# Two layers with adaptive norms on one core: layer 0's units ordered by batch row instead of by group

## The chip, the cores and the metric

One NeuronCore of a Trainium2 chip runs the whole computation in one program. The metric is the device time of one execution in microseconds, the median of several runs; one more execution was profiled. Everything is float32; where a matmul has to be exact, both operands are split into a rounded high part and a low remainder, and three fast matmuls (high-high, high-low, low-high) stand for one.

## The reference

Two layers are applied to x, two batch rows of 512 tokens with 512 channels. Each layer has an attention part and a feed-forward part, each behind a layer norm whose scale, shift and output gate come from a conditioning vector:

```python
mod = (silu(c) @ wmod).reshape(2, 6, 1, 512)          # sa, ca, ga, sb, cb, gb
h = layernorm(x) * (1 + ca) + sa;  x = x + ga * attn(h)
h = layernorm(x) * (1 + cb) + sb;  x = x + gb * ffn(h)
```

Layer 0's attention is a gated linear attention: 32 heads of 128 channels in 8 groups that share keys and values. A decay per token and head is worked out from h (`softplus(h @ Win.T + dt_bias)` times `-exp(A_log)`, summed up within chunks of 128 tokens). In each chunk the scores are weighted with the decays; a state of 128 x 128 per head is carried from chunk to chunk; the output is normalised, gated with `silu(h @ Wg.T)` and projected with `Wo`. Its feed-forward is one matmul with signs of a weight, times a scale, plus a bias.

Layer 1's attention is softmax attention with 32 heads of 16 channels over 512 tokens. Its feed-forward mixes four streams of 128 channels with a 4 x 4 matrix per token that 50 rounds of Sinkhorn normalisation make. The batch rows never meet.

## The kernel before

**Units.** Layer 0's attention is cut into 64 units; a unit is a group g of four heads, a batch row b and a chunk c of 128 tokens. Four units with the same g and b are a step. A list written out by hand gives the order of the steps: groups 0 to 3 alternate between the rows (group 0 row 0, group 0 row 1, group 1 row 0, ...), then come groups 4 to 7 of row 0, then groups 4 to 7 of row 1 (`AHEAD = 4`). So row 0 is finished at unit 47.

A pass of the loop over units issues: the scores of the next unit (`scores`, which fetches the summed decays `gb` from DRAM, spread over all partitions), the mix of this one (`mix`: `yps`, normalisation, gate `sg`), keys, queries and values of the next step (`project`, matmuls `pps`, rotation in `apply_rope`), the output projection of the unit before (`project_out`, 12 matmuls `ops`, added to the residual `xres`), the next unit's gate (`gps`), its state (`cps`), and the turned output (`ztp`, `zh`, `zl`).

**Weights.** A group needs 14 tiles of 128 x 512: `wk`, `wv`, four each of `wq`, `wg`, `wo`. Each is fetched by a DMA on SyncE's queue into a tile of the pool `raw` (four buffers), copied and rounded by ScalarE to the high part, and subtracted by GpSimd to the low part (lines 210 and 211), which frees the raw tile. With `raw_tile` other loads use the same pool: pieces of the modulation matrices (`mod_piece`: fetch two or four tiles, and at the next piece multiply those of the last one, `mps`), the feed-forward weight, the residual input. While rows alternate, a set of weights serves two steps, 8 units; in groups 4 to 7 one step.

**Decays.** `decays(b)` normalises the four tiles of a row, turns them (`ps_tr`), makes `hh` and `hl`, multiplies with `Win` (`zps`) and then works along rows of 32 partitions (lines 381 to 420): softplus, a running sum in 15 + 7 small adds, exponentials, three sets of transposes (`gtp`). It is called for row 0 ahead of the first keys and for row 1 after the first queries.

**Beside the units.** `tail(n)` is called in each pass. It issues modulation pieces at n % 8 in 3 to 6, and, once a row's units have all been projected, the feed-forward of that row in eight or nine passes: layer norm and modulation of tile c, sums, feed-forward of tile c - 2 (`fps`), layer 1's norm of tile c - 3, and at the end the key, value and query projections of layer 1. For row 0 these are passes 45 to 53, its weights coming from pass 42. The tail of row 1 goes on behind the last unit, in `virtual` passes.

**Layer 1.** 128 pieces (16 steps of 8). A piece issues two score matmuls with their row maxima (`maxima`, `s`, `m`), and ten pieces later the weights and exponentials for the same keys (`weigh`, `pt`); every four pieces make a quad, whose outputs (`op`) and division (`rc`) follow. From `FIRST = 53` on each unit's pass issues three pieces, up to `HOLD = 33`; the rest follow the last unit. Behind every eighth quad starts a Sinkhorn job (`streams`) for two tiles, which runs beside the further pieces; the last one ends the kernel.

**Order.** The instructions of every engine are put in order before the run by a list scheduler; priorities follow the order in the program, and `anchor`/`behind` tie work beside the units to its phase. On the chip every engine, SyncE with its DMA issues included, works its list strictly in order.

Of the kernel before, what the change touches and what calls it, by code (L numbers as in the profile page):

```python
# [12 lines left out]
PT, OUT = 16, 1  # L13
S1, S2, MT, OT, OP = 3, 3, 2, 2, 2
QS = 6
HOLD = 33
VECTOR = False, False, True, True
UPS = 400, 400, 400, 400
RATES = None, None, None, None
# [5 lines left out]
HL, RA, ZL, XC, XP = 0, 0, 100, 100, 1  # L25
UPO = 600
SPLIT0, SPLIT1 = 16, 16
AHEAD = 4
FIRST = 53
PER = 3  # L30
LATE, LATE1 = 2, 12
LAG = 10
# [5 lines left out]
P = 128  # L38
# [15 lines left out]
def tile_adaln(ctx: ExitStack, tc: tile.TileContext, a: dict, out: bass.AP):  # L54
# [5 lines left out]
    wk = ctx.enter_context(tc.tile_pool(name="wk", bufs=2))  # L60
    dram = ctx.enter_context(tc.tile_pool(name="dram", bufs=1, space=bass.MemoryType.DRAM))
    psp = ctx.enter_context(tc.tile_pool(name="ps", bufs=2, space=PSUM))


    table = nc.scalar.preload_act_table_set("natural_log_exp_and_others")
# [105 lines left out]
    def norm(src):  # L171
        xn = temp([P, HID], FP, "xn")
        normalised(xn, src)
        return xn
# [190 lines left out]
    cdb = keep([P, B * H0, NC])  # L365
    g_dram = [dram.tile([H0, L], FP, name=f"g_dram{b}") for b in range(B)]
    cd_dram = [dram.tile([H0, NC], FP, name=f"cd_dram{b}") for b in range(B)]
    def decays(b):

        zps = psp.tile([H0, L], FP, name="zps")  # L370

        def also(cs, ht):
            for kc in range(KC):
                nc.tensor.matmul(zps[:, cs], lhsT=win[:, kc, :], rhs=ht[:, kc, :], start=kc == 0, stop=kc == KC - 1)

        for c in range(NC):
            modulated(b, c, norm(xin[b * NC + c]), modT[0], 0, also=also)

        row = lambda n: temp([H0, L], FP, n)
        z, e, u, rest, dt = row("z"), row("e"), row("u"), row("rest"), row("dt")  # L380
        nc.vector.tensor_scalar(z, zps, dtb, None, ALU.add)
        nc.vector.scalar_tensor_tensor(e, z, -1.0, z, ALU.mult, ALU.min)
        act(e, e, AF.Exp)

        nc.vector.tensor_scalar(u, e, 1.0, None, ALU.add)
        nc.vector.scalar_tensor_tensor(rest, u, -1.0, e, ALU.add, ALU.subtract)
        act(dt, u, AF.Ln)
        act(u, dt, AF.Exp, scale=-1.0)
        nc.vector.tensor_tensor(rest, rest, u, ALU.mult)
        nc.vector.tensor_tensor(dt, dt, rest, ALU.subtract)  # L390
        nc.vector.scalar_tensor_tensor(dt, z, 0.0, dt, ALU.max, ALU.add)

        G = row("G")
        nc.vector.tensor_scalar(G, dt, alog, -1.0, ALU.mult, ALU.mult)
        Gb = G.rearrange("r (n i) -> r n i", i=16)
        for i in range(1, 16):
            nc.vector.tensor_tensor(Gb[:, :, i], Gb[:, :, i], Gb[:, :, i - 1], ALU.add)
        off = small.tile([H0, NC, 8], FP, name="off")
        G4 = G.rearrange("r (c n i) -> r c n i", n=8, i=16)
        nc.vector.memset(off[:, :, 0], 0.0)  # L400
        for n in range(1, 8):
            nc.vector.tensor_tensor(off[:, :, n], off[:, :, n - 1], G4[:, :, n - 1, 15], ALU.add)
        nc.vector.tensor_tensor(
            Gb, Gb, off.rearrange("r c n -> r (c n)").unsqueeze(2).to_broadcast([H0, NC * 8, 16]), ALU.add
        )
        nc.sync.dma_start(out=g_dram[b], in_=G)
        Gc = G.rearrange("r (c i) -> r c i", c=NC)
        glast = small.tile([H0, NC], FP, name="glast")
        nc.vector.tensor_copy(glast, Gc[:, :, P - 1])
        cd = small.tile([H0, NC], FP, name="cd")  # L410
        act(cd, glast, AF.Exp)
        nc.sync.dma_start(out=cd_dram[b], in_=cd)
        nc.sync.dma_start(out=cdb[:, b * H0:(b + 1) * H0, :], in_=cd_dram[b].partition_broadcast(P))

        nc.vector.tensor_tensor(
            e.rearrange("r (c i) -> r c i", c=NC), Gc, glast.unsqueeze(2).to_broadcast([H0, NC, P]), ALU.subtract
        )
        act(e, e, AF.Exp, scale=-1.0)
        nc.vector.tensor_tensor(e, e, dt, ALU.mult)
        nc.vector.tensor_scalar(G, G, -1.0, None, ALU.mult)  # L420
        for k, src in enumerate((G, dt, e)):
            tp = psp.tile([P, NC, H0], FP, name="gtp")
            for c in range(NC):
                nc.tensor.transpose(tp[:, c, :], src[:, c * P:(c + 1) * P], ident[0:H0, 0:H0])
            nc.scalar.copy(gcol[:, k, :, b * H0:(b + 1) * H0], tp)
# [261 lines left out]
    def project_q(b, t):  # L687
        rope_halves("wq1", t, t, b, q_dram[b][8 * t:8 * t + 8], (0, 16), (32,))

    ends = [(KV0 - AHEAD) * B * NC + AHEAD * NC - NC + 1, KV0 * B * NC - NC + 1]  # L690

    def tail(n):

        if n % 8 in (3, 4, 5, 6) and n < 40:
            mod_piece(load=n % 8 < 6)

        for b in range(B):
            c = n - ends[b]
            with behind():
                if -3 <= c < 1:  # L700
                    load_ffn(c + 3)
# [44 lines left out]
                ksd[j, s] = temp([P, L], FR, f"ks{j}{s}")  # L746
                nc.sync.dma_start(out=ksd[j, s].bitcast(FP), in_=empty.bitcast(FP))

    steps = [(g, b) for g in range(KV0 - AHEAD) for b in range(B)]
    steps += [(g, b) for b in range(B) for g in range(KV0 - AHEAD, KV0)]  # L750
    units = [{"at": (g, b, c)} for g, b in steps for c in range(NC)]

    def keys_of(s):
# [510 lines left out]
    for hh in range(REP0):  # L1264
        load_stationary("wq0", 0, hh)
    nc.sync.dma_start(out=rope, in_=a["c_rope0"].rearrange("p (k l) -> p k l", k=2))
    load_x(1)
    load_stationary("wv0", 0, 0)
    load_gate(0)
    load_out(0)  # L1270
    decays(0)
    keys_of(0)
    for hh in range(REP0):
        query_of(0, hh)
    vT = values_of(0)
    decays(1)
    scores(units[0])
    values_turned(0, vT)
    units[1]["st"] = state(units[0], None)
# [151 lines left out]
```

## Time and profile before

| | us |
|---|---|
| median of 3 runs | 1403.43 (1400.64 to 1406.42) |
| profiled execution, its own time | 1409.56 |
| span in the profile | 1407.8 |
| TensorE busy / VectorE busy | 1247.3 / 1164.4 |
| ScalarE busy / GpSimd busy | 825.1 / 787.2 |
| first output projection of layer 0 (unit 0, unit 32, unit 44) | at 109.8, 539.1, 691.7 |
| first score matmul of layer 1 | at 898.4 |
| end of layer 0's units | at about 1046 |
| sixteenth quad of layer 1 done (all of row 0) | at 1157 |
| last quad done | at 1279 |

PE is TensorE, PEld its weight loads, DVE VectorE, ACT ScalarE, POOL GpSimd, SP SyncE. The page has 40 slices of 35.2 us; a digit is the busy share in tenths. In lines of the stretches every engine's busy microseconds are followed by the number of its instructions. In lines of waits the total of the waits is followed by their number and the longest.

### The profile page before, as it was taken

What the parts mean: (1) busy time and instruction counts of PE and PEld (TensorE: products, weight loads), DVE (VectorE), ACT (ScalarE), POOL (GpSimd) and SP (SyncE); (2) the same over time, 40 slices, a digit from 0 to 9 for tenths busy, and PEclk for the clock granted to TensorE, in tenths of its full rate; (3) what the DMA queues carried; (4) which work ended last, traced back from release to release, by engine and by line L of the source; (5) the groups of instructions that cost most, each with busy time, mean ns of one, the idle gap of its engine ahead of it and who ended that gap; (6) DMA issues with size and microseconds to landing.
All of it is one profiled execution on the core that took longest, in us unless ns stands there. A gap on an engine that the chain in (4) does not pass through costs nothing. (4 is left out here: it accounts for less than half of the span.)

```text
span 1407.8 us, 23038 instructions
## 1 busy us (share of the span) xinstructions
PE 1247.3 (89%) x7128; PEld 990.5 (70%) x7128; DVE 1164.4 (83%) x3171; ACT 825.1 (59%) x2333; POOL 787.2 (56%) x1180
## 2 busy tenths in 40 slices
PE   6979999999999999999988998899998899994117
PEld 3767888788788778888876777677776667762116
DVE  7998668687677687787999977788699879888998
ACT  5456576476476466666665655567567467653226
POOL 4363274365264367577777757644243644657854
PEclk9999999999999999999999999999999899986568
DMA  7121241231131233224333327623212331100001
GB/s 241 36 70 43 87 124 39 68 106 53 53 118 56 94 117 111 81 79 128 120 106 90 98 70 233 179 66 97 65 42 94 101 92 48 59 2 1 1 15 46
DMA packets 95378, 117.14 MB, mean 83 GB/s; under 512 B 10828, under 2 KB 50508, under 8 KB 95256
## 3 DMA queue, kind: packets, MB, share of 16 engines
q1 hardware_dynamic: 95256, 115.67, 27.6%
q8 instruction: 57, 0.93, 0.3%
q14 instruction: 65, 0.53, 0.1%
HBM read 102.11 MB, written 10.64 MB: 80 GB/s over the span
## 5 line engine op out<-in xcount | busy, mean ns | idle before, releaser
L847 DVE TENSOR_REDUCE m<-s 128x1 f32<-128x512 f32 x256 | 166.6, 673 | 21.8 <-PE s L843 21.5
L68 ACT ACTIVATE pt<-s 128x512 f32<-128x512 f32 x256 | 137.4, 601 | 33.1 <-PE s L877 31.5
L448 POOL TENSOR_TENSOR q<-xcos,rot 128x512 f32<-128x512 f32 x64 | 92.8, 1450 | 56.5 <-DVE xcos L446 52.5
L68 ACT ACTIVATE sg<-sg 128x512 f32<-128x512 f32 x128 | 80.7, 632 | 64.5 <-DVE sg L479 62.5
L496 POOL TENSOR_SCALAR_AFFINE_SELECT dec<-gb 128x512 f32<-128x512 f32 x64 | 48.3, 755 | 121.2 <-DMA gb<-g_dram 65.4
L843 PE MATMUL s<-ks,qs 96*128 96x512 f32 x256 | 104.9, 442 | 11.5 <-DVE m L847 7.6
L877 PE MATMUL s<-qs,ks 100*128 100x256 f32 x512 | 104.4, 309 | 10.2 <-DMA qs<-mm 6.8
L233 PE MATMUL pps<-hh,wq_h 128*128 128x512 f32 x256 | 103.3, 403 | 7.1 <-ACT vT L767 3.4
L877 PEld LDWEIGHTS s<-qs,ks 100*128 100x128 f32 x512 | 82.7, 199 | 32.8 <-issue 7.9
L68 ACT ACTIVATE dec<-dec,room 128x128 f32<-128x128 f32 x256 | 83.0, 398 | 34.8 <-POOL dec L496 34.6
L233 PE MATMUL ops<-wo_h,zh 128*128 128x512 f32 x256 | 102.2, 399 | 1.2 <-ACT zh L571 1.0
L233 PE MATMUL gps<-wg_h,hh 128*128 128x512 f32 x256 | 101.3, 398 | 1.5 <-ACT wg_h L210 1.2
L233 PE MATMUL ops<-wo_h,zl 128*128 128x512 f32 x256 | 101.5, 396 | 0.7 <-DVE zl L572 0.7
L233 PE MATMUL pps<-hl,wq_h 128*128 128x512 f32 x256 | 101.8, 398 | 0.0
L233 PE MATMUL pps<-hh,wq_l 128*128 128x512 f32 x256 | 101.5, 397 | 0.0
L233 PE MATMUL gps<-wg_l,hh 128*128 128x512 f32 x256 | 101.1, 395 | 0.0
L233 PE MATMUL ops<-wo_l,zh 128*128 128x512 f32 x256 | 100.6, 393 | 0.0
L233 PE MATMUL gps<-wg_h,hl 128*128 128x512 f32 x256 | 100.6, 393 | 0.0
L516 POOL TENSOR_TENSOR gb<-gb,q 128x512 f32<-128x512 f32 x48 | 62.3, 1299 | 60.3 <-ACT gb L68 46.7
L549 PE MATMUL yps<-v,dec 128*128 128x128 f32 x512 | 93.4, 278 | 2.7 <-DVE xcos L446 1.4
L555 ACT ACTIVATE z<-yps 128x128 f32<-128x128 f32 x256 | 67.5, 278 | 41.1 <-PE yps L551 30.5
L559 DVE SCALAR_TENSOR_TENSOR z<-yps,ss,sg 128x128 f32<-128x128 f32 x256 | 72.0, 340 | 22.5 <-ACT ss L68 22.3
(321 smaller groups left out, 3984.4 us busy)
## 6 DMA issues: line engine op xcount, KB each, us to landing
gb<-g_dram SPq DMA_DIRECT2D x64, 256.0 KB
raw<-in_wq SPq DMA_DIRECT2D x56, 256.0 KB
raw<-in_wg SPq DMA_DIRECT2D x48, 256.0 KB
raw<-in_wo SPq DMA_DIRECT2D x48, 256.0 KB
raw<-in_wmod SPq DMA_DIRECT2D x40, 256.0 KB
qs<-q_dram SPq DMA_DIRECT2D x64, 96.0 KB
q_dram<-hi SPq DMA_DIRECT2D x16, 256.0 KB
raw<-in_wk SPq DMA_DIRECT2D x14, 256.0 KB
```

The lines of the kernel that those rows point to most:

```text
L68: ins = nc.scalar.activation(o, i, func, **kw)
L233: nc.tensor.matmul(ps, lhsT=l, rhs=r, start=i == 0, stop=i == n - 1)
L448: nc.gpsimd.tensor_tensor(dst, sp(xc_), sp(rot), ALU.add)
L496: anchor["pool"] = nc.gpsimd.affine_select(out=dec, in_=gb, pattern=[[0, REP0], [1, P]], compare_op=ALU.is_ge, fill=-1e30, base=0, channel ...
L516: nc.gpsimd.tensor_tensor(gb, gb, q[:, c], ALU.mult)
L549: nc.tensor.matmul(yps[:, h, :], lhsT=u["pr"][:, h, :], rhs=u["v"][:, c, :], start=True, stop=not c)
L555: nc.scalar.activation(z[:, h, :], yps[:, h, :], AF.Square, accum_out=ss[:, h:h + 1])
L559: nc.vector.scalar_tensor_tensor(z[:, h, :], yps[:, h, :], ss[:, h:h + 1], sg[:, h * P:(h + 1) * P], ALU.mult, ALU.mult)
L843: anchor["pe"] = nc.tensor.matmul(ps, lhsT=st["qs"][rp][0:KS, i, qt * P:(qt + 1) * P], rhs=st["ks"][s][0:KS], start=True, stop=True,).ins
L847: anchor["dve"] = nc.vector.tensor_reduce(st["m"][:, 2 * qt + s, i:i + 1], ps, AX.X, ALU.max, negate=True).ins
L877: nc.tensor.matmul(ps[:, j, :], lhsT=st["ks"][s][0:KM, kt * P:(kt + 1) * P], rhs=st["qs"][rp][0:KM, i, :], start=True, stop=True,)
```

## The change

Layer 0's steps go row by row: all eight groups of row 0 (units 0 to 31), then all of row 1 (units 32 to 63). Every step now brings a new group, so 16 sets of weights are fetched instead of 12, the second one's `wk`, `wq` and `wv` ahead of the loop.

`decays` is divided: `decays_tile` does one tile (and adds the bias to its own 128 columns), `decays_rest` the rows, `decays_columns` the transposes. Row 0's are called at the start as before; row 1's input is fetched in pass 5, its tiles are done in passes 7, 9, 11 and 13, its rows in 15 and its transposes in 17.

Modulation pieces come in every odd pass from 3 to 27. Row 0's feed-forward runs in every second pass from 24 on (weights from 24, first tile at 30, projections of layer 1 at 46). Layer 1 starts at unit 47 with three pieces a unit, up to 43. Row 1's feed-forward starts at the same unit as before. Tiles of whole multiples of 2 KB per partition are placed at multiples of 2 KB.

```diff
-HOLD = 33
+HOLD = 43
...
-AHEAD = 4
-FIRST = 53
+ROW0 = 24
+FIRST = 47
...
+    class Aligned:
...
+        def tile(self, shape, dt, **kw):
+            whole = int(np.prod(shape[1:])) * 4 % 2048 == 0
+            return self.pool.tile(shape, dt, **kw, **({"align_bytes": 2048} if whole else {}))
+
+    ck, raws, wts, wk = Aligned(ck), Aligned(raws), Aligned(wts), Aligned(wk)
...
-    def decays(b):
-
-        zps = psp.tile([H0, L], FP, name="zps")
+    row = lambda n: temp([H0, L], FP, n)
+    decay = {}
+
+
+    def decays_tile(b, c):
+        if c == 0:
+            decay["z"] = row("z")
 
         def also(cs, ht):
+            zps = psp.tile([H0, P], FP, name="zps")
             for kc in range(KC):
-                nc.tensor.matmul(zps[:, cs], lhsT=win[:, kc, :], rhs=ht[:, kc, :], start=kc == 0, stop=kc == KC - 1)
-
-        for c in range(NC):
-            modulated(b, c, norm(xin[b * NC + c]), modT[0], 0, also=also)
-
-        row = lambda n: temp([H0, L], FP, n)
-        z, e, u, rest, dt = row("z"), row("e"), row("u"), row("rest"), row("dt")
-        nc.vector.tensor_scalar(z, zps, dtb, None, ALU.add)
+                nc.tensor.matmul(zps, lhsT=win[:, kc, :], rhs=ht[:, kc, :], start=kc == 0, stop=kc == KC - 1)
+            nc.vector.tensor_scalar(decay["z"][:, cs], zps, dtb, None, ALU.add)
+
+        modulated(b, c, norm(xin[b * NC + c]), modT[0], 0, also=also)
+
+    def decays_rest(b, part):
+
+        if part:
+            return decays_columns(b, *decay["G"])
+        z, e, u, rest, dt = decay["z"], row("e"), row("u"), row("rest"), row("dt")
...
-        for k, src in enumerate((G, dt, e)):
+        decay["G"] = G, dt, e
+
+    def decays_columns(b, *rows):
+        for k, src in enumerate(rows):
...
-    ends = [(KV0 - AHEAD) * B * NC + AHEAD * NC - NC + 1, KV0 * B * NC - NC + 1]
-
     def tail(n):
 
-        if n % 8 in (3, 4, 5, 6) and n < 40:
-            mod_piece(load=n % 8 < 6)
+        if n % 2 and 3 <= n < 29:
+            mod_piece(load=n < 27)
+        if n == 5:
+            load_x(1)
+        if n in (7, 9, 11, 13):
+            decays_tile(1, (n - 7) // 2)
+        if n in (15, 17):
+            decays_rest(1, (n - 15) // 2)
 
         for b in range(B):
-            c = n - ends[b]
+            if b:
+                c = n - len(units) + NC - 1
+            elif n % 2 or n >= len(units):
+                continue
+            else:
+                c = (n - ROW0) // 2 - 3
...
-    steps = [(g, b) for g in range(KV0 - AHEAD) for b in range(B)]
-    steps += [(g, b) for b in range(B) for g in range(KV0 - AHEAD, KV0)]
+    steps = [(g, b) for b in range(B) for g in range(KV0)]
...
-    load_x(1)
     load_stationary("wv0", 0, 0)
     load_gate(0)
     load_out(0)
-    decays(0)
+    for c in range(NC):
+        decays_tile(0, c)
+    for part in range(2):
+        decays_rest(0, part)
     keys_of(0)
+    load_stationary("wk0", 1, 0)
     for hh in range(REP0):
         query_of(0, hh)
+        load_stationary("wq0", 1, hh)
     vT = values_of(0)
-    decays(1)
+    load_stationary("wv0", 1, 0)
     scores(units[0])
```

## The prediction

> **What bounds the kernel now.** First the page, for which engine is full and where.
>
> ```profile
> PE 1247.3 (89%) x7128; PEld 990.5 (70%) x7128; DVE 1164.4 (83%) x3171; ACT 825.1 (59%) x2333; POOL 787.2 (56%) x1180
> PE   6979999999999999999988998899998899994117
> DVE  7998668687677687787999977788699879888998
> ```
>
> TensorE is full from the fourth slice on; VectorE stands at nine tenths in the third and fourth slice and again in four slices behind the middle, and in just those TensorE drops. So the next view was the busy time by stretch, with bounds put where these digits change.
>
> ```profile
> 0.00:110.00 110.00, 87.22 (x418) 62.52 (x419) 98.25 (x245) 55.56 (x149) 51.43 (x42) 0.97 0.38 114
> 110.00:540.00 430.00, 426.21 (x2190) 346.71 (x2189) 316.95 (x656) 259.64 (x766) 211.94 (x178) 1.00 0.27 81
> 540.00:690.00 150.00, 149.71 (x779) 127.07 (x778) 124.31 (x239) 101.00 (x294) 106.84 (x87) 1.00 0.33 96
> 690.00:842.00 152.00, 139.04 (x682) 114.89 (x681) 138.91 (x268) 89.86 (x263) 104.00 (x83) 0.97 0.33 95
> 842.00:905.00 63.00, 53.99 (x243) 41.41 (x243) 45.72 (x75) 33.65 (x85) 45.80 (x39) 0.97 0.74 229
> 905.00:1046.00 141.00, 133.59 (x832) 105.29 (x830) 121.16 (x271) 90.22 (x258) 56.90 (x54) 0.96 0.23 66
> 1046.00:1157.00 111.00, 101.18 (x751) 72.54 (x752) 98.57 (x262) 69.63 (x167) 55.52 (x105) 0.94 0.30 95
> ```
>
> The columns behind the length are TensorE, its weight loads, VectorE, ScalarE, GpSimd, clock, DMA share, GB/s. Layer 0's units run from 110 to 1046. At 110 to 690 TensorE lacks 4.1 us in 580: nothing but its own work counts there. It lacks 22.8 at the start, 13.0 at 690 to 842 (row 0's feed-forward in a few units; VectorE at 91%), 9.0 at 842 to 905 (layer 1 starts, DMA at 0.74), 7.4 and 9.8 behind that. Matmuls are neither added nor taken away, so the change can only win or lose such idle time. Behind the sixteenth quad of layer 1 (1157, half of its 32) the built programs have the same VectorE work in the same place, and nothing of the change reaches there: the last 247 us are taken as they are.
>
> The third view is TensorE's waits from 26 (first key projection) to 126 (third unit), 12.8 us in all; the three longest:
>
> ```profile
> PE pps L233 <- ACT vT L767: 3.4, 1, 3.4
> PE pps L233 <- DVE xcos L446: 2.6, 1, 2.6
> PE gtp L424 <- DVE xcos L446: 1.9, 2, 1.7
> ```
>
> **Start: row 1's decays leave it.** The order of the built program shows how far. Row 1's four normalisations, its 16 transposes and 24 of its 32 small `zps` matmuls stay at the start; only the decay rows (L381 to L420), 8 `zps` and 12 `gtp` move into units 9 to 17. In the groups of that stretch these VectorE rows sum, for both rows of the batch, to 11.6 (L397) + 5.0 (L402) + 2.4 + 2.2 + 2.2 + 2.0 + 1.8 + 1.5 + four of 1.3 + three of 0.8 = 36.3 us; half is 18.2. VectorE is busy 98 of 110 us there, so 18 us less of it should take most of the 12.8. Not all: keys and queries still come through the same engine, and three more weight loads are put in front. Between 0 and 12.8 I take 9, nearer the upper end because the wait lines name VectorE. Four small `zps` adds for one, 3 x about 0.2, are within this. Later, in units 9 to 17, the 18 us lie beside TensorE.
>
> **Weights: 16 sets of 14 instead of 12.** 56 more loads, ScalarE copies (0.61) and GpSimd subtractions (1.29): 34 and 72 us, all in units 0 to 31, where a group now lasts 4 units and not 8. Units 32 to 43 already work so today. There a unit is (691.7 - 539.1)/12 = 12.7 us, VectorE has 124.31/11.8 = 10.5 of it, GpSimd 9.1, against 13.4, 9.9 and 6.6 in units 0 to 31 (with the modulation matmuls). TensorE covers all of it: 0. If VectorE were the bound, the 0.6 us more per unit would cost 19.
>
> ```profile
> L397 DVE TENSOR_TENSOR G<-G x30: 193/206/1293, 52.6 to 96.1; 32x32 f32<-32x32 f32 x30
> L211 POOL TENSOR_TENSOR wq_l<-raw,wq_h x48: 1258/1292/2725, 14.3 to 879.9; 128x512 fp32r<-128x512 f32 x48
> ```
>
> Why VectorE grows at all is in these two: a 32x32 add takes 193 ns, and 1293 at worst, the length of one GpSimd subtraction. The Trainium skill has a rule for this that speaks against the change (SBUF — State Buffer, "Who interferes with whom"): a VectorE instruction with two SBUF inputs and a GpSimd one that reads SBUF exclude each other for a whole instruction. By the rule each of the 56 subtractions could hold up VectorE for its length, 72 us by the row's 1.29, and with VectorE as the bound the sum would be that much worse. The rows of units 32 to 43 measured 0.6 a unit, under TensorE's cover.
>
> **The ring of raw tiles.** Weights and modulation pieces share the pool `raw` of four. A modulation piece keeps its tiles until its matmuls; these come one unit after the load now, two units after it in the changed kernel, in which weights are also wanted twice as often.
>
> ```profile
> 390.76 1.06 PE L272 MATMUL mps<-raw,room 128*32 128x512 f32 x8
> 391.84 0.34 SPq L201 DMA_DIRECT2D raw<-in_wg  x1
> 577.18 0.33 SPq L201 DMA_DIRECT2D raw<-in_wo  x1
> 580.79 5.05 POOL L211 TENSOR_TENSOR wo_l<-raw,wo_h 128x512 fp32r<-128x512 f32 x4 [2.40 <-ACT wo_h L210]
> 587.17 0.19 PEld L233 LDWEIGHTS ops<-wo_h,zh 128*128 128x128 f32 x1
> ```
>
> Today a weight load starts the moment the modulation matmuls end, and `wo` is ready 1.3 us before its use. In the built order of the changed kernel the new group's `wk`, `wq` and `wo` stand on SP's queue behind the modulation's matmuls at units 4, 8, 20 and 24, and behind them wait the next `gb` loads, which are two units ahead. From the first such matmul: 0.3 to free a tile, 2.9 from issue to the copy, 0.6 copy, then GpSimd: six subtractions and two `xw` between them, 8 x 1.3 = 10.4: 14.2 us until the last `wo`. TensorE has 1.06 + 9.8 us of other matmuls in front of the output projection and 2.0 in it: 12.9. Short by 1.3 at each of four changes: +5. Lower end 0 (slack is 1.3 today and none was lost); upper end, if the five adds and products of GpSimd that stand about there (6.4 us) come first, 7.7 x 4 = +31.
>
> **Row 0's feed-forward over units 30 to 46.** Now it lies in units 44 to 52 (691.7 to 841.8). Over nine units of 10.5 and 12.7 it adds 138.9 - 94.5 = 44 us of VectorE and 139.0 - 114.3 = 25 of TensorE. Over 17 units that makes VectorE 178.5 + 44 = 223 and TensorE 216 + 25 = 241: 0.93 of TensorE's work, where it is 1.00 now. At 0.90 (650 to 700) TensorE lost 0.6%, at 1.00 9%; on the line between, 0.93 is 3.1%, 7.5 us against 13.0: -6. Ends: 0 (a straight line from 0.83 gives 5.5%, as much as is lost now) and -13.
>
> **Layer 1 from unit 47, 43 pieces in layer 0.** Ten pieces of about 1.6 us of TensorE (two score matmuls of 0.24, four of 0.12, a quarter of 1.86 for the outputs, small ones) move from a stretch that loses 8.8% to one that loses 5.2%: -1, ends ±6, because row 1's feed-forward then has ten pieces fewer beside it. The start of layer 1 keeps its 9.0. The 2 KB alignment has no price in a row: the 48 subtractions above differ by 3% between smallest and median, wherever their tiles lay: 0, ±3.
>
> **Sum.** -9 + 0 + 5 - 6 - 1 = -11 us on the profiled execution's own 1409.56 (span 1407.8): 1398.6. The median of the runs shown is 1403.43, 0.9957 of it: 1392.5, rounded 1392. The terms' ends, taken together at about two thirds: -33 and +20.
>
> **Rivals.** *Waits at the group change* (slower): place, the first output projection of units 4, 8, 20 and 24; without the ring term the gain is 16, so it decides from 4.0 us per change; at 7.7 it is +31 - 16 = +15, 1424.6, or 1418. For it: four tiles for six loads, 1.3 us of slack today. Against: 9.8 us of other matmuls stand in front of each, and no such wait shows today. *Spreading wins nothing* (no change): VectorE at 0.93 and then three pieces a unit loses as much as two crowded stretches do, and the start gives half: -4.5 + 5 - 1 = -0.5, 1403. For it: at 905 to 1046 VectorE is at 86% and TensorE still loses 5.2%. *Row 1's decays hardly move* is true in part, since only 18 of their us leave the start; if those were covered anyway, 9 is 0, and the sum -2, 1401.
>
> **How the numbers follow.** A measurement of this kernel can tell about 0.5%, 7 us: under 1396 is faster, over 1410 slower. Forecast, with all terms near the values taken: 0.52. The two no-change cases: 0.22. Waits at the group change, or more lost in the crowded units than the rows say: 0.26. The range goes from 1370 (-33) to 1414, part of the way into the first rival.
>
> **What would show it.** Start: the first output projection, at 109.8 now, some 10 us earlier; TensorE's waits up to the third unit near 4 us instead of 12.8. Units 30 to 46: VectorE under 95% with TensorE over 96%. Ring: waits `ops <- wo_l`, 1 to 2 us at four changes; over 4 us each refutes the sum. Same 247 us behind the sixteenth quad, else the tail was not untouched. Layer 0's end would stay within about 10 us of 1046, although it holds 16 us more of layer 1.

## The result, and the profile after

The changed kernel takes 1463.44 us (1462.23 to 1466.32), the kernel before on the same chip 1404.93: a ratio of 1.0406, 95% interval 1.0373 to 1.0438. It is 57 us slower by this ratio, where 1392 had been forecast. The profiled execution spans 1462.4 us. One execution of one experiment below took 3129 us, twice its others, and is left out of that run's median and ratio.

Below, first from the page of the changed kernel, how full the engines are, and TensorE and VectorE by slices (36.6 us each now):

```profile
PE 1261.8 (86%) x7128; PEld 990.0 (68%) x7128; DVE 1178.0 (81%) x3177; ACT 856.7 (59%) x2389; POOL 861.4 (59%) x1236
...
PE   6889999899999989999998789999999859995116
...
DVE  7977778787768899889966596776879769898998
```

TensorE's own work is the same 7128 matmuls, 14 us longer than before; the rest of the loss, 40 us, is idle time. Its digits drop in three places: at the start, at slices 22 to 24 (layer 1 starts), and at slices 32 and 33 (behind the last unit). The second view is the busy time by stretch, cut at the places in the program that answer to the stretches before (columns as there: TensorE, weight loads, VectorE, ScalarE, GpSimd, clock, DMA share, GB/s):

```profile
0.00:103.00 103.00, 77.19 (x356) 55.99 (x357) 87.79 (x209) 55.20 (x147) 57.41 (x46) 0.92 0.43 131
103.00:329.00 226.00, 217.71 (x1109) 174.44 (x1108) 177.61 (x364) 142.83 (x412) 139.20 (x113) 1.00 0.35 105
329.00:455.00 126.00, 126.00 (x640) 98.39 (x639) 89.77 (x181) 73.73 (x213) 68.88 (x57) 1.00 0.34 101
455.00:571.00 116.00, 105.25 (x508) 82.52 (x507) 103.66 (x189) 71.94 (x208) 92.09 (x74) 0.99 0.45 134
571.00:739.00 168.00, 164.53 (x840) 137.19 (x839) 149.34 (x287) 112.62 (x323) 114.97 (x93) 1.00 0.30 89
739.00:845.00 106.00, 90.26 (x424) 73.80 (x422) 62.28 (x122) 56.85 (x151) 63.13 (x54) 0.94 0.50 156
845.00:1092.00 247.00, 233.12 (x1369) 183.99 (x1370) 189.65 (x411) 154.03 (x424) 116.53 (x112) 0.97 0.26 78
1092.00:1212.00 120.00, 95.52 (x651) 67.36 (x651) 92.79 (x260) 64.85 (x163) 57.37 (x107) 0.90 0.24 75
1212.00:1462.00 250.00, 152.25 (x1242) 116.30 (x1241) 225.09 (x1159) 124.64 (x356) 151.83 (x586) 0.80 0.09 26
```

The first output projection is at 103.4 (109.8 before), unit 32's at 570.5 (539.1), unit 44's at 739.0 (691.7), the last unit's at 1091.8 (1031.2), the sixteenth quad at 1212 (1157), the end at 1462. So 31 us are lost up to unit 32, 16 between units 32 and 44, 13 more to the last unit, and 5 us are won back before the sixteenth quad. Not all of this is comparable work: ten pieces of layer 1 moved into the units. Up to the sixteenth quad TensorE idles 102 us (the differences of the first two numbers, added up) instead of 66. Behind it 250 us are left, as before (251 of the profile's span of 1407.8).

Third view, TensorE's waits from 26 to 114 (first key projection to second unit), the longest three:

```profile
PE gtp L445 <- DVE xcos L467: 3.1, 1, 3.1
PE pps L244 <- DVE off L420: 3.0, 1, 3.0
PE pps L244 <- DVE hh L201: 2.4, 1, 2.4
```

All waits of this window sum to 14.1 us, up to the third unit (127.7) as well, and their releasers are still VectorE's rows, now those of row 0's own decays (`off`) and of its modulated input (`hh`). Fourth, the waits at the start of layer 1 (739 to 845), TensorE's and then ScalarE's, and those behind the last unit (1092 to 1212):

```profile
PE cps L244 <- ACT vT L796: 7.4, 1, 7.4
```

```profile
ACT hi L774 <- DMA q_dram<-hi: 7.0, 1, 7.0
```

```profile
PE s L872 <- DMA qs<-q_dram: 14.4, 1, 14.4
```

ScalarE stood 7.0 us in front of the padding of layer 1's keys (L774), whose buffer the rotated queries' DMA still held, and behind it in its queue stood the copy `vT`, for which TensorE waited 7.4. The longest wait of all, 14.4 us, is for row 1's queries. The chain in order of time names each hop of it (start, length, what):

```profile
1166.69 5.88 DMA k_dram<-lo
...
1175.04 5.01 DMA q_dram<-hi
...
1183.92 5.12 DMA qs<-q_dram
```

Row 1's rotated keys and queries are written to DRAM (5.9 and 5.0 us) and fetched again (5.1), and only then can the next score matmul run. And the wait costs more than its length; the granted clock right behind it:

```profile
1189.00:1193.00 4.00, 3.83 (x10) 1.91 (x14) 3.03 (x6) 0.00 (x0) 0.47 (x3) 0.50 0.47 118
1193.00:1197.00 4.00, 4.00 (x36) 1.93 (x29) 1.68 (x7) 0.37 (x1) 2.26 (x11) 0.63 0.51 172
1197.00:1201.00 4.00, 3.77 (x25) 2.56 (x27) 3.85 (x12) 2.82 (x5) 2.12 (x9) 1.00 0.60 223
```

It is 0.50 for 4 us and 0.63 for the next 4: some 3.5 us of clock (4 x 0.50 + 4 x 0.37) on top of 14.4. If the clock is either half or whole, as the other lines have it, it was half for about 7 us behind the wait. The Trainium skill (TensorE: Matmul & The Clock Gate, "Part 1: The HAM clock gate") says that TensorE falls to half its clock after at least one idle window of about 3.4 us and gets it back after at least one busy one. The first of these lines agrees with the half, and the 7 us are two such windows and not one.

### The profile page after: what moved, and what is told of

It is laid out like the page before. It is cut to its first block, busy times and chain, and to the rows that moved or that the text cites. A ratio compares the mean times of both kernels' runs of the same rounds, so it can differ in the third digit from the quotient of the medians.

```text
span 1462.4 us, 23335 instructions
## 1 busy us (share of the span) xinstructions
PE 1261.8 (86%) x7128; PEld 990.0 (68%) x7128; DVE 1178.0 (81%) x3177; ACT 856.7 (59%) x2389; POOL 861.4 (59%) x1236
## 4 chain that ended last, share of the span: by engine, by line
PE 28%; DVE 19%; POOL 8%; DMA 7%; ACT 5%; issue 4%; SPq 1%; POOLq 0%; DVEq 0%; ACTq 0%
PE pps L244 6%; PE ops L244 4%; PE gps L244 3%; PE op L926 3%; DVE m L876 3%; PE s L906 3%; PE s L872 2%; DMA qs<-mm 1%; DMA gb<-g_dram 1%; PE yps L570 1%; POOL sinkhorn L1141 1%; POOL wq_l L222 1%; POOL sinkhorn L1142 1%; PE sps L244 1%; DVE ql L476 1%
## 5 line engine op out<-in xcount | busy, mean ns | idle before, releaser
L872 PE MATMUL s<-ks,qs 96*128 96x512 f32 x256 | 102.4, 441 | 24.4 <-DMA qs<-q_dram 14.4
L244 PE MATMUL gps<-wg_h,hh 128*128 128x512 f32 x256 | 101.6, 399 | 5.2 <-DVE xres L608 1.8
L222 POOL TENSOR_TENSOR wg_l<-raw,wg_h 128x512 fp32r<-128x512 f32 x64 | 95.5, 1512 | 12.8 <-ACT wg_h L221 10.3
L222 POOL TENSOR_TENSOR wo_l<-raw,wo_h 128x512 fp32r<-128x512 f32 x64 | 87.9, 1391 | 16.1 <-ACT wo_h L221 12.4
L222 POOL TENSOR_TENSOR wq_l<-raw,wq_h 128x512 fp32r<-128x512 f32 x64 | 87.2, 1366 | 16.5 <-ACT wq_h L221 14.8
L517 POOL TENSOR_SCALAR_AFFINE_SELECT dec<-gb 128x512 f32<-128x512 f32 x64 | 43.6, 682 | 89.0 <-DMA gb<-g_dram 66.4
```

What stands on the lines that cost most here:

```text
L222: nc.gpsimd.tensor_tensor(lo, raw, hi.bitcast(FP), ALU.subtract)
L244: nc.tensor.matmul(ps, lhsT=l, rhs=r, start=i == 0, stop=i == n - 1)
L517: anchor["pool"] = nc.gpsimd.affine_select(out=dec, in_=gb, pattern=[[0, REP0], [1, P]], compare_op=ALU.is_ge, fill=-1e30, base=0, channel ...
L872: anchor["pe"] = nc.tensor.matmul(ps, lhsT=st["qs"][rp][0:KS, i, qt * P:(qt + 1) * P], rhs=st["ks"][s][0:KS], start=True, stop=True,).ins
```

## The experiments

Medians of three to ten runs each; the ratio is to the kernel before on the same chip, with its 95% interval. The table, called the ladder below, builds the change up from the kernel before, one edit at a time; each line holds all edits above it.

| kernel | us | ratio | step, us |
|---|---|---|---|
| before + 2 KB placement | 1401.6 | 0.9982 (0.9963 to 1.0001) | -2.5 |
| + row by row (AHEAD = 8) | 1411.5 | 1.0048 (1.0024 to 1.0072) | +9.3 |
| + second group's six loads ahead | 1417.0 | 1.0107 (1.0084 to 1.0130) | +8.3 |
| + row 1's decays in passes 5 to 17 | 1413.2 | 1.0075 (1.0048 to 1.0103) | -4.5 |
| + row 0's feed-forward spread | 1416.7 | 1.0084 (1.0053 to 1.0116) | +1.3 |
| + modulation pieces spread | 1430.9 | 1.0188 (1.0157 to 1.0219) | +14.6 |
| + FIRST = 47 | 1452.7 | 1.0330 (1.0313 to 1.0346) | +19.9 |
| + HOLD = 43 (the changed kernel) | 1463.4 | 1.0406 (1.0373 to 1.0438) | +10.7 |

A step is the difference of two ratios times 1404.9. They sum to 57.0, by construction. Steps under about 5 us are within what two such intervals leave open. One order of adding the edits was run; in another order a step can differ, as the one of the modulation pieces does below.

**Placement.**

```diff
+    ck, raws, wts, wk = Aligned(ck), Aligned(raws), Aligned(wts), Aligned(wk)
```

> The kernel before with the 2 KB placement alone. Theory (placement has no price): within 4 us of the kernel before. Rival (it moves tiles so that engines wait longer on each other): 5 us or more slower, which would be part of every other run here.

1401.6. It costs nothing, and can be left in all the others.

**The order alone.**

```diff
-AHEAD = 4
+AHEAD = 8
```

> The kernel before (median 1404.9) with only AHEAD = 8, so that its units go row by row with 16 sets of weights, and the 2 KB placement, without which it does not fit in SBUF; modulation pieces, row 1's decays at the start, feed-forward of row 0 in consecutive passes, FIRST = 53 and HOLD = 33 stay as before. Theory (the order and its 56 more weight loads slow units 0 to 31): unit 32's output projection at 560 to 575 instead of 539, total 1425 to 1445. Rival (it is what the change puts beside the units, not the order): unit 32 within 8 us of 539, total 1398 to 1412.

1411.5. Here the second step still uses the first group's key, query and value weights (six loads fewer); the next kernel has them. Of the 31 us lost up to unit 32 the order makes 12 (551 instead of 539), ten of them behind unit 24 (425.2 against 423.0), where row 0's feed-forward now begins.

**Order with all loads.**

```diff
     keys_of(0)
+    load_stationary("wk0", 1, 0)
     for hh in range(REP0):
         query_of(0, hh)
+        load_stationary("wq0", 1, hh)
     vT = values_of(0)
+    load_stationary("wv0", 1, 0)
```

> As the run with the order alone, but with the second group's keys, queries and values weights loaded ahead of the loop as in the changed kernel; that run used the first group's for the second step and so had 6 of 224 loads less. Theory (loads cost little): within 4 us of that run's 1411.5. Rival (six loads in front of the decays hold GpSimd and so VectorE at the start): first output projection 5 us or more behind 111.5, total 1417 to 1422.

1417.0: the rival's total. The six loads cost 8 us by the ratios and 5.5 by the medians (the kernel before measured 1405.8 beside the one and 1401.9 beside the other), though not at the first output projection (112.8): unit 8 is at 214.6 instead of 209.1. The 50 further loads are another matter; the stretch from unit 8 to unit 24 in the kernel before and here:

```profile
204.80:423.00 218.20, 218.20 (x1117) 178.22 (x1115) 163.04 (x334) 127.97 (x378) 105.30 (x88) 1.00 0.25 73
```

```profile
214.60:430.70 216.10, 216.10 (x1117) 177.99 (x1117) 170.76 (x334) 141.51 (x404) 144.61 (x117) 1.00 0.36 108
```

With 29 more instructions on GpSimd VectorE needs 7.7 us more, and TensorE is still busy to the last microsecond: 216.1 us for the same 1117 matmuls.

**Order and decays.** The changed kernel with the four other edits taken back:

```diff
-HOLD = 43
+HOLD = 33
-FIRST = 47
+FIRST = 53
...
-        if n % 2 and 3 <= n < 29:
-            mod_piece(load=n < 27)
+        if n % 8 in (3, 4, 5, 6) and n < 40:
+            mod_piece(load=n % 8 < 6)
...
-            elif n % 2 or n >= len(units):
+            elif n >= len(units):
                 continue
             else:
-                c = (n - ROW0) // 2 - 3
+                c = n - 29
```

> The changed kernel with the pieces, the feed-forward's passes (first tile at pass 29), FIRST = 53 and HOLD = 33 as in the kernel before: only the order, the loads and row 1's decays moved into passes 5 to 17 are left of the change. Theory of the prediction (moving the decays wins the start): 6 to 9 us faster than the order alone, 1402 to 1406. Rival (what the start wins, units 5 to 17 lose): 1409 to 1416. Rival (they cost more beside the units): 1420 to 1430, with the loss between units 8 and 20.

1413.2. The first output projection is 11.2 us earlier (101.6 instead of 112.8), and units 8 to 24 give it back:

```profile
204.10:431.60 227.50, 222.09 (x1142) 179.75 (x1141) 190.16 (x375) 143.13 (x412) 147.05 (x117) 1.00 0.35 104
```

```profile
PE pps L244 <- DVE st L559: 2.9, 1, 2.9
```

11.4 us longer than the line before it. TensorE is busy 6.0 us longer: row 1's decays bring 16 `zps` and 12 `gtp` here, 3.2 us from start to next start, and the others are the same matmuls taking longer. 5.4 us are idle, in waits on VectorE that were not there; the longest is shown.

**Feed-forward spread.** The last of these four edits not taken back:

```diff
-            elif n >= len(units):
+            elif n % 2 or n >= len(units):
                 continue
             else:
-                c = n - 29
+                c = (n - ROW0) // 2 - 3
```

> The changed kernel with HOLD = 33, FIRST = 53 and the modulation pieces as before; order, loads, moved decays and row 0's feed-forward over units 30 to 46 are left of the change. It differs by the feed-forward's passes alone from the run with order and decays, 1413. Theory of the prediction (spreading saves 6): 1403 to 1409. Rival (spreading wins nothing): 1410 to 1416. Rival (spreading costs): 1418 or more.

1416.7: nothing is won. In the units that the consecutive passes had crowded the loss falls; it comes back where the spread passes end, with the projections in pass 46. Units 32 to 42 and 42 to 48, consecutive and spread:

```profile
560.00:738.00 178.00, 163.87 (x811) 134.25 (x810) 146.32 (x271) 110.67 (x322) 126.89 (x101) 0.99 0.39 116
738.00:813.00 75.00, 75.00 (x391) 63.71 (x390) 62.09 (x128) 52.17 (x154) 49.67 (x41) 1.00 0.29 87
```

```profile
567.00:702.00 135.00, 131.75 (x681) 110.11 (x680) 120.77 (x232) 94.22 (x275) 99.19 (x79) 1.00 0.28 84
702.00:814.00 112.00, 101.48 (x480) 84.73 (x479) 76.22 (x151) 65.51 (x182) 72.67 (x57) 0.94 0.43 130
```

TensorE idles 14.1 and 0 us in the one, 3.3 and 10.5 in the other. A second run from the other side, the changed kernel with consecutive passes:

```diff
-            elif n % 2 or n >= len(units):
+            elif n >= len(units):
                 continue
             else:
-                c = (n - ROW0) // 2 - 3
+                c = n - 38
```

> The changed kernel with row 0's feed-forward in consecutive passes from 38, its projections in pass 46 as in the changed kernel. Theory of the prediction (spreading saves): 3 to 8 us slower, 1466 to 1471. Rival (spreading costs, since units 24 to 48 took 390 us where the order alone with consecutive passes had 381): 5 to 9 us faster, 1454 to 1458. If neither matters: within 3 us of 1463.

1464.6, ratio 1.0445 (1.0398 to 1.0492): no difference that can be told.

**Modulation pieces.** Three runs. First `FIRST = 53` and `HOLD = 33` in the changed kernel, to be compared with the spread feed-forward above for the pieces and with the next paragraph for FIRST:

```diff
-HOLD = 43
+HOLD = 33
-FIRST = 47
+FIRST = 53
```

> The changed kernel with HOLD = 33 and FIRST = 53 as before (to be compared with HOLD = 33 alone, 1452.7). Theory (layer 1's start in the units in which row 0's feed-forward ends and the next weights are fetched costs 15 to 25 of TensorE's time): 1428 to 1438. Rival (the start costs the same six units later): 1448 to 1456.

1430.9. Then the pieces' old schedule in the changed kernel:

```diff
-        if n % 2 and 3 <= n < 29:
-            mod_piece(load=n < 27)
+        if n % 8 in (3, 4, 5, 6) and n < 40:
+            mod_piece(load=n % 8 < 6)
```

> The changed kernel with the modulation pieces on the schedule of before (four passes of eight, so a piece's matmuls come one unit after its load). Units 8 to 24 take 238.5 us in the changed kernel and 218 before (216 with the order alone changed). Theory (spread pieces hold the raw tiles two units each and starve the weight loads): units 8 to 24 in 218 to 226 us, total 1445 to 1452. Rival (row 1's decays, or VectorE's own load, are the loss there): units 8 to 24 within 4 us of 238, total 1459 to 1467.

1451.5, ratio 1.0353 (1.0329 to 1.0377), with units 8 to 24 in 229.8. Then the spread pieces, each multiplied one pass after its load:

```diff
-        if n % 2 and 3 <= n < 29:
-            mod_piece(load=n < 27)
+        if 3 <= n < 28:
+            mod_piece(load=n % 2)
```

> The changed kernel, its modulation pieces still spread over passes 3 to 27, but a piece's matmuls one pass after its load and not two, so that a piece holds its raw tiles for one unit. Theory (the ring of raw tiles is what the spread pieces cost): about as good as the pieces' old schedule, 1450 to 1455. Rival (it is the pieces' spacing or the other work beside them, not the time for which they hold the ring): 1459 to 1467.

1453.3, ratio 1.0352 (1.0327 to 1.0377): as good as the old schedule. So the spacing is harmless, and the second unit for which a piece holds its raw tiles costs some 7 us here, and the spread pieces 15 on the ladder. The traces show in part where this pair differs. First all engines from unit 0 to unit 44, in the changed kernel and with one unit's hold; then the modulation matmuls alone from 100 to 571 (the time in which at least one of them runs):

```profile
103.40:739.00 635.60, 613.10 (x3090) 492.50 (x3090) 519.98 (x1019) 400.72 (x1153) 415.14 (x333) 1.00 0.35 105
```

```profile
101.20:726.80 625.60, 606.56 (x3091) 491.78 (x3090) 524.53 (x1019) 398.98 (x1153) 413.94 (x333) 1.00 0.35 107
```

```profile
100.00:571.00 471.00, 20.01 (x80) 2.75 (x80) 8.12 (x12) 1.00 0.37 111
```

```profile
100.00:571.00 471.00, 14.82 (x80) 2.10 (x80) 8.13 (x12) 1.00 0.38 114
```

Of the 10 us between the first two lines 6.5 are TensorE's busy time and 3.5 idle. The same 80 modulation matmuls take 5.2 us more, since the four column tiles of a piece (four matmuls of 32 columns that run at once) more often stand apart in TensorE's list. That is most of this pair's difference, but not a price of the spread pieces as such: the 80 take 20.0 us in the kernel with order and decays too, 22.1 in the one with order and loads and 15.9 in the kernel before. On the ladder the step from 17.9 to 20.7 makes 3 of the 15 us; 9 are idle time.

No line of TensorE's waits in these units names a weight tile, only VectorE's rows. SyncE's queue, the other suspect, shows this from 104 to 450, in the changed kernel and with one unit's hold:

```profile
SPq L212 <- PE mps L283: 55.2, 10, 16.7
SPq L515 <- PE yps L572: 50.9, 4, 22.7
```

```profile
SPq L212 <- PE mps L283: 88.6, 9, 21.2
SPq L515 <- PE yps L572: 4.9, 5, 2.6
```

A load of `gb` holds the queue, with the weight loads behind it, for up to 22.7 us instead of 2.6; but the waits for the modulation matmuls are longer in the better kernel, and all waits of the queue sum to 290 us in the one and 283 in the other. So the queue is not shown to be what costs, and the rest of the ladder's step stays open.

**HOLD.**

```diff
-HOLD = 43
+HOLD = 33
```

> The changed kernel with HOLD back at 33, so that 31 pieces of row 0 instead of 21 are left when layer 0 ends (its own median 1463.4). Theory (row 1's tail comes too late): the 14.4 us wait of TensorE for row 1's queries falls under 3 us, the last unit starts about 16 us earlier (1076 instead of 1092), and the total falls by 12 to 16, to 1447 to 1451. Rival (the ten pieces only change places, and TensorE waits elsewhere for VectorE): the total stays within 4 us of 1463.

1452.7, and the wait for row 1's queries is shorter, not gone (waits from 1074 to 1200):

```profile
PE s L872 <- DMA qs<-q_dram: 6.0, 1, 6.0
```

Behind the last unit (to the sixteenth quad) TensorE now idles 14.7 us; in the changed kernel, whose line is second, 24.5:

```profile
1074.00:1197.00 123.00, 108.31 (x774) 77.70 (x776) 108.14 (x276) 72.78 (x178) 54.78 (x88) 0.94 0.27 84
```

```profile
1092.00:1210.00 118.00, 93.52 (x637) 65.61 (x637) 91.32 (x256) 63.20 (x159) 57.05 (x106) 0.90 0.24 77
```

These 9.8 us, 8.4 of them in the wait for row 1's queries, are about the 10.7.

**FIRST.** The step of 20 us is the largest. Is it the shared buffer?

```diff
-            empty = temp([P, L], FR, "hi1")
+            empty = temp([P, L], FR, "empty", 1)
```

> The changed kernel with a tile of its own for the padding of layer 1's keys, which shared the two buffers of hi1 with the rotated queries. Theory (the shared buffer makes ScalarE wait and TensorE with it): TensorE's wait cps for vT of 7.4 us goes, units 44 to 48 take 92 to 99 us instead of 106, total 1449 to 1456. Rival (the transfers themselves are late, whatever buffer): units 44 to 48 within 4 us of 106, total 1459 to 1467.

1457.9, ratio 1.0370 (1.0332 to 1.0409): units 44 to 48 take 93 us instead of 106 and the wait for `vT` is gone, but units 48 to 63 take 259 instead of 246. Some 5 us stay, within what the intervals leave open. Is it the nearness to row 0's projections (pass 46)? The run with order and decays, whose projections come at pass 37, with `FIRST = 47`:

```diff
-FIRST = 53
+FIRST = 47
```

> The run with order and decays (1413.2) with FIRST = 47 instead of 53, HOLD = 33 kept: row 0's feed-forward and its projections end nine passes before layer 1 starts. Theory (what costs 22 us is that layer 1 starts one pass behind row 0's projections): 1408 to 1417. Rival (an early start costs as such, its keys and queries beside the units' weight loads): 1428 to 1440.

1435.7, ratio 1.0204 (1.0169 to 1.0239): the same 18 us without that nearness. Then, from the same kernel, two pieces a unit from 47 and two a unit from 42:

```diff
-FIRST = 53
-PER = 3
+FIRST = 47
+PER = 2
```

> The run with order and decays with FIRST = 47 and two pieces of layer 1 a unit instead of three (33 pieces up to the last unit). Theory (VectorE is less crowded with two pieces a unit, and TensorE waits less in units 47 to 63): 5 to 10 us under 1413, 1402 to 1409. Rival (the pieces cost the same wherever they stand): 1410 to 1416.

1412.9, ratio 1.0043 (1.0022 to 1.0063): the early start costs nothing if it goes on slowly.

```diff
-FIRST = 53
-PER = 3
+FIRST = 42
+PER = 2
```

> The same with FIRST = 42, so that the 33 pieces are done by unit 58, before row 1's feed-forward begins. Theory (crowding): 1398 to 1408, better than FIRST = 47 with two. Rival (the last units then have nothing of layer 1 to fill TensorE while row 1's feed-forward keeps VectorE busy): 1413 to 1422.

1441.7, ratio 1.0254 (1.0205 to 1.0303): the worst of the four, at the rate that cost nothing from 47 on. What the two slow ones share is where layer 1's pieces run out: with three a unit from 47 the 33 pieces of HOLD are issued by unit 57, with two from 42 by unit 58, and row 1's feed-forward begins in pass 58 with its weights. The matmuls of layer 1's scores alone (first number behind the length) from unit 58 to the last unit: FIRST = 47 with three a unit, with two a unit, and FIRST = 53:

```profile
1010.00:1058.00 48.00, 5.98 (x23) 3.89 (x23) 5.74 (x9) 4.02 (x7) 0.97 0.23 72
```

```profile
983.00:1041.00 58.00, 13.15 (x59) 9.27 (x60) 11.68 (x18) 10.04 (x19) 1.00 0.19 62
```

```profile
971.00:1039.00 68.00, 18.75 (x84) 12.76 (x84) 17.67 (x28) 13.64 (x25) 1.00 0.21 67
```

There 6 us of score matmuls lie where the others have 13 and 19. For all engines, from unit 42 to unit 58, to the last unit and to the sixteenth quad, three a unit and two a unit from 47:

```profile
739.00:1010.00 271.00, 261.05 (x1423) 213.29 (x1422) 211.25 (x421) 171.81 (x468) 141.90 (x125) 0.96 0.31 95
1010.00:1058.00 48.00, 44.53 (x257) 35.69 (x256) 44.87 (x99) 31.05 (x100) 23.39 (x19) 0.97 0.23 72
1058.00:1180.00 122.00, 110.02 (x770) 79.31 (x772) 106.36 (x276) 72.75 (x177) 55.16 (x88) 0.92 0.27 84
```

```profile
740.00:983.00 243.00, 236.82 (x1272) 195.96 (x1271) 198.64 (x391) 157.66 (x433) 141.01 (x120) 0.99 0.33 103
983.00:1041.00 58.00, 56.85 (x361) 46.20 (x361) 49.06 (x122) 40.99 (x128) 22.16 (x22) 1.00 0.19 62
1041.00:1162.00 121.00, 112.67 (x825) 80.73 (x823) 111.35 (x288) 74.86 (x183) 59.12 (x102) 0.94 0.29 90
```

For nearly the same work (2450 and 2458 matmuls in 441 and 422 us) TensorE idles 25.4 us instead of 15.7, and is busy 415.6 instead of 406.4, at a granted clock of 0.96, 0.97 and 0.92 where the other has 0.99, 1.00 and 0.94. Half of the 19 us is idle time, half is busy time at a lower clock. And the running out is only part of it: of the 9.7 us of idle time 3.8 lie ahead of unit 58, while pieces are still issued, and there the lower clock weighs most (271 us x 0.04 = 11 us, against 243 x 0.01 = 2). With three a unit, TensorE's largest wait ahead of unit 58 and its two largest behind it:

```profile
PE s L872 <- DVE m L876: 7.0, 6, 1.6
```

```profile
PE s L872 <- DMA qs<-q_dram: 4.3, 1, 4.3
PE s L906 <- DMA qs<-mm: 2.9, 1, 2.9
```

So three a unit cost twice: while they are issued, TensorE's score matmuls wait for VectorE's row maxima (7.0 us, where two a unit have 0.6); once they have run out, they wait for the DMAs of row 1's queries (7.2 us, where two a unit have no such wait in the list). With two a unit from 42 TensorE idles 11.3 us from unit 42 to 58, 4.1 to the last unit and 17.2 behind it, where the same rate from 47 has 6.2, 1.2 and 8.3: there the running out is the larger part. Last, two a unit in the changed kernel itself:

```diff
-PER = 3
+PER = 2
```

> The changed kernel with two pieces of layer 1 a unit instead of three, all else kept (FIRST = 47; by the last unit 34 pieces are done, so HOLD = 43 is not reached). Theory (three a unit from 47 use row 0's pieces up too early, and none are left to fill TensorE under row 1's feed-forward): as good as FIRST = 53 with HOLD = 33, 1426 to 1434, with the 14.4 us wait for row 1's queries gone. Rival (the start one pass behind row 0's projections costs it, whatever the rate): 1445 to 1455, the gain of HOLD = 33 alone.

1439.7 beside 1408.9 on its chip, ratio 1.0211 (1.0184 to 1.0238): 27 of the 31 us of FIRST and HOLD together, as good within the intervals as FIRST = 53 with HOLD = 33 (1.0188). Its profile still has the wait for `vT` (7.5 us) and 6.7 of the one for row 1's queries, which had been expected to go. So the start right behind row 0's projections is the smaller part of the cost.

**From the other side: decays and loads.** Row 1's decays back at the start of the changed kernel:

```diff
+    load_x(1)
     load_stationary("wv0", 0, 0)
...
     vT = values_of(0)
+    for c in range(NC):
+        decays_tile(1, c)
+    for part in range(2):
+        decays_rest(1, part)
     load_stationary("wv0", 1, 0)
```

> The changed kernel with row 1's input and decays back at the start (behind the first values). Theory (moved decays only won the start): first output projection 5 to 10 us later than 103.4, all else as in the changed kernel, total 1468 to 1473. Rival (beside units 7 to 17 they cost as much as at the start or more): unit 16 at 320 to 330 in spite of the later start, total 1452 to 1464.

1484.0, ratio 1.0544 (1.0521 to 1.0567): both expectations missed. Units 8 to 24 are 12 us shorter, but the first output projection comes at 135.7, 32 later. The kernel with order and loads has the same decays and the same loads at the start and its first output projection at 112.8; what differs there is the decays' cutting into tiles. How that makes 23 us was not followed, and stays open. And 12 sets of weights in the changed kernel; it leaves out the loads of row 0's odd groups, which work with the weights of the group before:

```diff
+    def fresh(s):
+        return s >= KV0 or s % 2 == 0
...
-            more = steps[s + 2][0] if s + 2 < len(steps) and steps[s + 2][0] != steps[s + 1][0] else None
+            more = steps[s + 2][0] if s + 2 < len(steps) and fresh(s + 2) else None
...
-            if units[n - 1]["at"][0] != g:
+            if units[n - 1]["at"][0] != g and fresh(s):
                 load_out(g)
```

> The changed kernel without the weight loads of row 0's odd groups (these use the weights of the even group before; 12 sets as in the kernel before). Theory (56 more loads are the loss in units 0 to 31): unit 32 at 538 to 548 instead of 570, total 1432 to 1442. Rival (the modulation pieces and row 1's decays in units 3 to 27 are the loss): unit 32 at 560 or later, total 1453 or more.

1446.9, ratio 1.0291 (1.0262 to 1.0320): between the two. 9 of the 16 us are there at the first output projection (94.1), the other 7 by unit 32 (554.3 instead of 570.5). So beside the pieces and the decays the 50 loads in the loop are not free.

**A milder order.** In the kernel before, with the placement:

```diff
-AHEAD = 4
+AHEAD = 6
```

> The kernel before with the 2 KB placement and AHEAD = 6: groups 0 and 1 alternate between the rows, then groups 2 to 7 of row 0, then of row 1 (14 sets of weights, none ahead of the loop; row 0's feed-forward at passes 37 to 45, layer 1 from 53). Theory (row 0's feed-forward well ahead of layer 1's start wins, the loads cost nothing): 1393 to 1401. Rival (as with AHEAD = 8, it costs a few us): 1405 to 1413.

1406.3 beside 1408.9, ratio 0.9981 (0.9969 to 0.9994). It is the only kernel whose interval stays below 1, by 3 us, which is the placement's own share. So no version was found that beats the kernel before by more than 0.2%.

## Why the prediction was wrong, step by step

**Right:** that the stretch behind the sixteenth quad stays (250 us, and 251 in the profile before; the 247 of the prediction are the median less 1157), and that the further loads cost TensorE nothing in units 8 to 24 of the kernel with order and loads. Half right: that only TensorE's idle time can change. It makes 36 of the 55 us up to the sixteenth quad; the others are the same matmuls taking longer, at a lower clock or in modulation matmuls that stand apart (20.0 us instead of 15.9); how much is due to which was not worked out. The prediction had put each subtraction at up to its whole 1.29 us of VectorE, by the skill's rule about the shared port (SBUF — State Buffer, "Who interferes with whom"). In units 8 to 24, where GpSimd has 29 instructions more, VectorE's 334 take 7.7 us longer, 0.27 for each, and TensorE loses nothing. The rule is in line with a rise; the worst case that the prediction worked out from it is five times the measured one. No run separated it from what the same loads bring to ScalarE and the DMA.

**Start, -9.** The sign of the milestone was right (-6.4 instead of -10), its meaning was not. TensorE idles 25.8 us up to it instead of 22.8; the stretch is shorter because it holds 10 us less of matmuls. The failing sentence is "Later, in units 9 to 17, the 18 us lie beside TensorE": of the 11.2 us that the decays' move wins at the start, 11.4 come back in units 8 to 24, over half of it (6.0) as busy time of TensorE, 3.2 of that in row 1's own small matmuls (16 `zps`, where the prediction had read 8, and 12 `gtp`), which the sum left out since "matmuls are neither added nor taken away". They were taken from a stretch in which TensorE idles into one in which it is full. And the loads "put in front", six and not three, cost 8, where the sum had them within the 9. Both together: +4 instead of -9. The waits stayed at 14.1 instead of falling to 4.

**Weights, 0.** Right for units 8 to 24 with order and loads alone; in the changed kernel the 50 loads in the loop cost about 7 us by the run with 12 sets. The order's own +9 was not in the sum: row 0's feed-forward now meets a row whose units each carry their own loads, and TensorE lacks 22 us in units 24 to 44 of the kernel with order and loads. That the two are cause and effect was not isolated.

**Ring, +5.** The longer hold does cost, more than was said (+15 on the ladder, 7 by the runs in the changed kernel), but not by the mechanism of the sum: no wait `ops <- wo_l` shows at the changes of group, and SyncE's queue stands as long with the short hold. 5 of the 10 us between the two traces are the modulation matmuls themselves; the rest is not explained.

**Feed-forward, -6.** Its sign was half met. Over units 30 to 46, the stretch that the prediction named, VectorE is at 83% and TensorE at 95%, under the 96 asked for:

```profile
535.90:802.90 267.00, 253.78 (x1273) 209.88 (x1274) 221.60 (x434) 176.50 (x510) 185.00 (x151) 0.99 0.33 102
```

VectorE's work, 222 us, is the sum's 223, but TensorE idles 13.2 us where the sum had 7.5, which is just the 13.0 of the crowded units before. The failing step is the line drawn through two stretches of different make-up: the spread stretch loses less in its middle and hands the loss on to the units at its end. Nothing was won: +1.3, and no difference from the other side. The rival "spreading wins nothing" was right here.

**Layer 1 from unit 47 with 43 pieces, -1 ± 6.** This is the term that decided: +19.9 and +10.7, more than half of the 57. Two of its steps failed. "The start of layer 1 keeps its 9.0": TensorE idles 15.7 us there (739 to 845), 7.4 of them in the wait for `vT`. And the sum priced ten pieces by the share of time that the stretches lose, as if a piece were work. It is filler as well: row 0's 64 pieces are all there is to put under the end of row 1's layer 0, its feed-forward, its projections and their way through DRAM. The phrase "because row 1's feed-forward then has ten pieces fewer beside it" had the mechanism in it, and gave it 6 us. FIRST = 47 with three a unit crowds the units in which it spends the filler and lacks it behind them, and HOLD = 43 leaves 21 pieces for a tail whose chain has three transfers of 5 to 6 us in a row: 24.5 us of idle time behind the last unit instead of 14.7.

**Rivals.** The rival on the slower side that had a place and a price was the ring at four places, and no time went there. The 0.26 also took in "more lost in the crowded units than the rows say", which is part of what came, but without a place or a price. "Layer 0's end would stay within about 10 us of 1046" was the sign that failed most plainly: the last unit starts 61 us later.

## What to carry to other kernels

Price a moved instruction on every engine at both ends: what leaves a stretch in which the bounding engine idles and enters one in which it is full costs its length there, however small it is, and can bring new waits with it (here 6.0 us busy and 5.4 idle). Count the filler that later, latency-bound stretches need before starting it earlier: start and rate together set where it runs out (two a unit cost nothing from unit 47 and 25 us from unit 42), and a high rate crowds the units in which it is spent. And build a change of many edits up one edit at a time: here two constants made 31 of 57 us, and the reordering with its loads 18.

## What was not expected of the hardware

An idle microsecond of TensorE can cost nearly a second one through the granted clock: in one pair of kernels 9.7 us more idle came with 9.2 us more busy time for nearly the same matmuls, at a lower granted clock, and behind a wait of 14.4 us the clock stood at 0.50 for 4 us. It does not always: HOLD = 33 takes 9.8 us of idle time away behind the last unit, and the whole falls by 10.7. And matmuls of four column tiles cost by their neighbours: the same 80 took 14.8 us where they mostly stood together and 20.0 where others more often stood between them.
